# A recurrent GRU kernel: the input weights loaded in twelve 128-row chunks by GpSimd's queue, with the head of the program put in another order

## The chip, the cores and the metric

The kernel runs on one core of a Trainium2 chip. A core has five engines with instruction queues of their own: TensorE (PE in the profile; its weight loads are PEld), VectorE (DVE), ScalarE (ACT), GpSimd (POOL) and SyncE (SP). Each engine works through its queue in program order, and waits on semaphores where an operand comes from elsewhere. Transfers between the chip's memory (DRAM) and the on-chip memory (SBUF) are issued from the queues of SP, ACT or POOL and run on 16 DMA engines. Matmul results land in PSUM, which has eight banks.

The metric is the device time of one execution in microseconds. Less is better.

## The reference

A gated recurrent unit runs over 128 steps for a batch of 64, with 512 inputs and 512 hidden values, all in float32, and its outputs are added to x:

```
def step(h, inp):
    x_t, prop = inp
    comb = concatenate([x_t, h], -1)
    z = sigmoid(comb @ Wz + bz)
    r = sigmoid(comb @ Wr + br)
    comb2 = concatenate([x_t, r * h], -1)
    h_cand = tanh(comb2 @ Wh + bh)
    h_new = (1 - z) * h + z * h_cand
    h_next = where(prop, tanh(h_new @ Wp + bp), h_new)   # prop: every 4th step but the last
    return h_next, h_new
out = x + transpose(scan(step, h0, transpose(x)))
```

Each of Wz, Wr, Wh is 1024 x 512: the upper 512 rows multiply x and the lower 512 rows multiply h (or r * h). The state h0 is the input cond_1024.

## The kernel before

**Gates and halves.** The three gates are R, Z and H. `wx` holds the upper (x) halves of the three weight matrices as [128 partitions, 4 chunks k, 3 gates, 512], and `wh[R]`, `wh[Z]`, `wh[H_]` hold the lower (h) halves, one tile for each gate. Partition p = 32 q + e of chunk k holds row 128 q + 32 k + e of the matrix, for four quarters q. The batch is cut into two halves of 32. A gate's product for one half is four `products` (one for each chunk k), each of them two matmul calls, which the profile shows as four float32 matmuls 128x256. In this text a *unit* is one such `products` call: one chunk, one gate, one half, four matmuls. A recurrent gate (`gate`, L218) is four units for each half.

**Recurrent work.** `half(h)` (L782) is a generator that emits one half's steps: gate R, then rh = r * h_old and its transpose, gate Z, some fill, gate H, the new state and its transpose, some fill; and behind every fourth step a product with Wp. The loop at the end of the function runs the two generators against each other, the second one `LAG` = 700 columns behind, so that one half's products cover the other half's elementwise chain. The order that comes out is the order of every engine's queue; no scheduler changes it (`manual_schedule`).

**Fill work.** The products with x do not depend on the state. They stand in a list `queue`, `put` appends to it, and `fill(n, h)` takes the next n units for half h. `HEAD`, `PLACES` and `TAIL` hold how many units each step takes at its three places. For the first four steps these are plain products (`plain`, L434: three gates x four chunks for each half of the batch and step, in the PSUM tiles scratch_q and scratch_r for even steps, scratch_a and scratch_x for odd ones); `add_bias` (DVE, L417) then adds the bias into `cp`, and `seed` (ACT, L379) copies `cp` into the PSUM tile in which the recurrent gate accumulates. From step 4 on, groups of x products are done with fewer multiplications, by matmuls of 192 columns (`batch`): seven products stand for eight, on sums of blocks of x and of blocks of the weights.

**The sums that this needs.** Sums of x blocks: `sum_raw12(1)` makes the tile s12r, `sum_raw34(1)` the tile s34r, four POOL operations 128x128 each. Sums of weight blocks: `sum_inner(i, eng)` and `sum_inner_1(i, eng)` make, for factor i, four operands from four operations 128x384 (L297 to L302), and `sum_outer` (L288 to L290, six operations 128x768 into `tw`) and `sum_outer_1` (L294, two into `d5`) make the factors 4 to 7 out of `wx`. Step 1's fill is `batch((1, 0), ...)` on factors 1 and 2 with s12r; step 2's is `batch((1, 1), ...)` on factors 1, 5, 2 and 3 with s12r and s34r, then `batch((1, 2), ...)`; from step 3 on come the factors 6, 7 and 4.

**The head.** Ahead of step 0 the program is straight code. Transfers: x of steps 0 and 1 and all of `wx` on SP and ACT (`load_x`, L94; `load_w`, L100, one transfer for each quarter of 32 partitions); the biases, then h0, on POOL, which is held by a copy that waits for `wx`; x of steps 2 and 3 on SP; then `wh` on SP and ACT, and x of later steps and Wp on SP (`later_loads`). Compute: PE runs 40 fill matmuls on zeros (`idle`), spreads the biases over the partitions (`spread`, L181, with copies on ACT, L189), then 8 and 8 more fill matmuls around the transposes of x (`join_x`, DVE, L251). DVE turns h0 and makes the sums of factors 1 and 2 while POOL makes `d5` and the sums of 3 and 5. PE runs the plain products of steps 0 and 1, R of both, then Z of both, then H of both. Then the six `add_bias` (emitted when H of step 0 and of step 1 ends), the seeds, and step 0. In step 0 DVE runs `sum_outer`, and POOL `sum_raw12(1)` and the sums of 6.

Lines that the text names: L123 and L128 are the POOL transfers of biases and h0, L126 the copy into `held`, L610 `bias_d`, L757 the add of h to x, L551 and L546 sums of results, L799 rh, L838 and L847 the new state, L238 the transposes of states.

## Time and profile before

| | |
|---|---|
| median of 3 runs | 1277.14 us (1275.61 to 1277.23) |
| profiled execution | 1276.41 us, of which the profile's span is 1274.6 us |
| PE, PEld busy | 1253.5 us (98%), 1164.3 us (91%) |
| DVE, ACT, POOL busy | 781.5, 835.6, 886.8 us |
| mean granted PE clock | 0.994 of full speed |
| DMA | 60.82 MB, mean 48 GB/s |

A time line row has the start in microseconds from the span's beginning, the time from its first to its last instruction, the engine, the line, the operation, the output and inputs by tile name, the shape and the count; square brackets hold the idle time ahead of it and what ended it. Matmuls are pipelined, so the spacing of their starts, not the time of one, is what one costs. A row of waits has the waiting engine and operation, what released it, the sum in us, the number of waits and the longest. A window row has its length and each engine's busy time in it, then the clock that PE was granted (1.00 is full), the share of the 16 DMA engines' time that was busy (transfers that overlap on one engine can bring it over 1) and GB/s. A wait for several semaphores is put down to the one that came last by the profile, and may belong to another.

### The profile page before, as it was taken

The numbers are of one execution on the slowest core, as the hardware profiler recorded it, in microseconds if no ns is written. First come the engines' busy times: TensorE is split into PE (matmuls) and PEld (weight loads), VectorE is DVE, ScalarE is ACT, GpSimd is POOL, SyncE is SP. The second block draws the span as 40 slices with busy tenths as digits, with TensorE's granted clock in tenths as the row PEclk, the third lists the DMA queues.
The fourth block names the chain that finished last, engine by engine and source line by source line (L and its number), as shares of the span: only waits on it lengthen the run. The fifth ranks groups of instructions, "written<-read, shape, count | busy, mean of one in ns | idle before, by whom it ended". The sixth has DMA issues, their size and how long they took to land.

```text
span 1274.6 us, 60714 instructions
## 1 busy us (share of the span) xinstructions
PE 1253.5 (98%) x25968; PEld 1164.3 (91%) x25968; DVE 781.5 (61%) x2161; ACT 835.6 (66%) x2685; POOL 886.8 (70%) x1027
## 2 busy tenths in 40 slices
PE   6999999999999999999999999999999999999997
PEld 3699999999999999999999999999999999999875
DVE  4656666666666666666666665666666666666544
ACT  1456667666667666666766666666666666667665
POOL 5469767787677786777687677776777777677530
PEclk8999999999999999999999999999999999999999
DMA  8302212102121111112111121111111111111010
GB/s 225 83 20 53 52 37 54 49 22 52 51 54 36 34 46 44 52 36 54 36 34 52 49 54 39 32 40 52 52 37 36 52 37 52 40 49 36 9 46 19
DMA packets 113365, 60.82 MB, mean 48 GB/s; under 512 B 12969, under 2 KB 109481, under 8 KB 113097
## 3 DMA queue, kind: packets, MB, share of 16 engines
q1 hardware_dynamic: 110628, 53.46, 16.1%
q8 instruction: 205, 3.36, 1.2%
q10 hardware_dynamic: 2212, 3.34, 0.9%
q14 instruction: 64, 0.52, 0.1%
q0 software_dynamic: 256, 0.14, 0.1%
HBM read 40.11 MB, written 16.78 MB: 45 GB/s over the span
## 4 chain that ended last, share of the span: by engine, by line
PE 95%; DMA 2%; ACT 1%; issue 1%; DVE 1%; SPq 0%; ACTq 0%; POOLq 0%; POOL 0%; DVEq 0%
PE rec L209 44%; PE rec_z L209 16%; PE scratch_r L209 13%; PE scratch_q L209 10%; PE scratch_a L209 5%; PE scratch_y L209 4%; PE scratch_x L209 4%; DMA wx<-in_L_cond_Wh_dram 1%; DMA wh<-in_L_cond_Wh_dram 1%; SPq L94 0%; DMA wx<-in_L_cond_Wr_dram 0%; DMA wh<-in_L_cond_Wr_dram 0%; ACT rec_z L235 0%; ACT c L235 0%; DMA xr<-in_x_dram 0%
## 5 line engine op out<-in xcount | busy, mean ns | idle before, releaser
L209 PE MATMUL rec<-wh,rhT 128*32 128x256 f32 x4096 | 375.3, 379 | 0.1
L209 PE MATMUL rec<-wh,hT 128*32 128x256 f32 x3072 | 281.5, 379 | 1.3 <-DVE hT L238 1.3
L209 PE MATMUL rec_z<-wh,hT 128*32 128x256 f32 x3072 | 281.5, 379 | 0.1
L209 PEld LDWEIGHTS rec<-wh,rhT 128*32 128x32 f32 x4096 | 250.4, 110 | 20.0 <-ACT scratch_r L235 0.7
L235 ACT ACTIVATE scratch_r<-rec 64x128 f32<-64x128 f32 x512 | 128.0, 250 | 131.9 <-PE rec L209 67.9
L379 ACT COPY rec<-cp 64x256 f32<-64x256 f32 x512 | 189.9, 371 | 37.2 <-DVE cp L417 17.8
L209 PEld LDWEIGHTS rec<-wh,hT 128*32 128x32 f32 x3072 | 187.0, 110 | 15.2 <-ACT c L235 3.2
L209 PEld LDWEIGHTS rec_z<-wh,hT 128*32 128x32 f32 x3072 | 193.4, 110 | 7.3 <-ACT rec_z L379 0.6
L235 ACT ACTIVATE rec_z<-rec_z 64x128 f32<-64x128 f32 x512 | 128.0, 250 | 95.9 <-PE rec_z L209 83.8
L235 ACT ACTIVATE c<-rec 64x128 f32<-64x128 f32 x512 | 139.3, 272 | 62.2 <-PE rec L209 50.8
L757 POOL TENSOR_TENSOR xr<-xr,h 128x256 f32<-128x256 f32 x127 | 93.1, 734 | 93.1 <-DVE h L847 90.3
L546 POOL TENSOR_TENSOR mb<-mb,mb 128x768 f32<-128x768 f32 x58 | 106.2, 1831 | 66.9 <-DVE mb L512 66.9
L546 POOL TENSOR_TENSOR cp<-mb,mb 128x768 f32<-128x768 f32 x76 | 139.0, 1828 | 8.1 <-DVE mb L512 4.4
L546 POOL TENSOR_TENSOR cp<-mb 128x768 f32<-128x768 f32 x46 | 84.3, 1832 | 56.9 <-ACT rec_z L379 55.5
L813 DVE SCALAR_TENSOR_TENSOR keep<-rec_z,h 128x256 f32<-128x256 f32 x96 | 40.8, 425 | 133.6 <-ACT rec_z L235 130.5
L209 PE MATMUL scratch_r<-tw,s 128*32 128x192 f32 x928 | 120.9, 326 | 0.0
L485 ACT COPY cq<-scratch_q 128x384 f32<-128x384 f32 x212 | 102.1, 482 | 19.8 <-PE scratch_q L209 18.3
L502 DVE TENSOR_TENSOR cx<-scratch_r,cx 128x384 f32<-128x384 f32 x106 | 59.1, 558 | 80.6 <-PE scratch_r L209 69.3
L209 PE MATMUL scratch_q<-tt,s 128*32 128x192 f32 x928 | 103.7, 326 | 0.0
L508 DVE TENSOR_TENSOR mb<-scratch_q,cx 128x384 f32<-128x384 f32 x106 | 59.1, 557 | 57.9 <-ACT cq L485 57.7
L799 DVE TENSOR_TENSOR rh<-scratch_r,h 128x128 f32<-128x128 f32 x192 | 56.1, 292 | 60.0 <-ACT scratch_r L235 60.0
L209 PE MATMUL rec<-wh,hpT 128*32 128x256 f32 x992 | 91.4, 379 | 0.1
(182 smaller groups left out, 3823.9 us busy)
## 6 DMA issues: line engine op xcount, KB each, us to landing
out_dram<-xr SPq DMA_DIRECT2D x249, 64.0 KB, 1.8
xr<-in_x_dram SPq DMA_DIRECT2D x248, 64.0 KB, 2.1
xs<-in_x_dram SPq DMA_DIRECT2D x240, 64.0 KB, 2.2
wp<-in_L_cond_Wp_dram SPq DMA_DIRECT2D x4, 256.0 KB, 6.2
wx<-in_L_cond_Wr_dram SPq DMA_DIRECT2D x4, 128.0 KB, 3.1
wx<-in_L_cond_Wr_dram ACTq DMA_DIRECT2D x4, 128.0 KB, 3.6
wx<-in_L_cond_Wz_dram SPq DMA_DIRECT2D x2, 256.0 KB, 7.8
wx<-in_L_cond_Wz_dram ACTq DMA_DIRECT2D x2, 256.0 KB, 8.5
```

The lines of the kernel that those rows point to most:

```text
L209: nc.tensor.matmul(ps[part(2 * h + c)], lhsT=left, rhs=rhs(c), start=start, stop=True, skip_group_check=True,)
L235: nc.scalar.activation(dst[ts(d, 2 * V)], gate_ps(i, h)[ts(h, 2 * V), d, :], func)
L379: nc.scalar.copy(gate_ps(i, h)[rows].rearrange("p d (c n) -> p d c n", c=C), G[t][rows, :, :, i, :].rearrange("p c d n -> p d c n"),)
L485: nc.scalar.copy(c[:, :nm], ps[:, :nm])
L502: nc.vector.tensor_add(T2[what][:, :nm], r_ps[:, :nm], T2[what][:, :nm])
L508: nc.vector.tensor_add(blocks(1, 1), runs(q_ps[:, :nm]), runs(T2[what][:, :nm]))
L546: nc.gpsimd.tensor_add(dst, a, b)
L757: nc.gpsimd.tensor_add(xr[g][:, j], xr[g][:, j], h_new)
L799: nc.vector.tensor_mul(rh[:, h, :], r_, h_old[:, h, :])
L813: nc.vector.scalar_tensor_tensor(out=keep, in0=z, scalar=1.0, in1=h_old, op0=ALU.subtract, op1=ALU.mult)
```

## The change

**Loads.** The x half of each weight matrix comes in four transfers, one for each chunk k, each over all 128 partitions (256 KB), issued on POOL's queue: twelve in all, in the order R, Z, H. The biases move from POOL's queue to ACT's, h0 from POOL's to SP's ahead of x of steps 2 and 3. A memset on POOL writes one column of `wh[R]` behind the twelve issues; the transfers into `wh[R]` on SP and ACT have to wait for it. `wh[Z]` is issued behind the seeds of R, `wh[H_]` behind those of H.

**Order of the head.** The 16 fill matmuls and their places go. PE runs R of steps 0 and 1 first, then the spread of the biases, Z of both, H of both, and R of step 2. `add_bias` and the seeds of a gate follow that gate's products. Of the weight sums only those of factor 1 stay ahead of step 0 (on DVE).

**Weight sums.** In step 0, behind gate R, DVE makes those of 2; POOL, held by a copy that waits for them, makes those of 3 and `d5`, then behind gate Z s12r and the sums of 5; at the end of the step POOL makes `sum_outer`, which DVE did before. The sums of 6 move from step 0 to step 1, behind s34r, those of 7 from step 1 to step 3. Step 0 takes eight fill units for each half ahead of gate Z, and (4, 8, 0) instead of (12, 12, 0) at its places; x products of steps 2 and 3 are as many as before.

```
--- before.py
+++ after.py
@@ -114,25 +114,32 @@
     bias_p = const.tile([P, S, J], F32, name="bias_p")
     new_xr(0)
     load_x(xr[0], 0, 2, engs=both_queues)
-    for k in range(0, K, 2):
-        load_w(wx[:, :, R, :], gates_in[R][:D], k, k + 2, both_queues)
-    for i in (Z, H_):
-        load_w(wx[:, :, i, :], gates_in[i][:D], engs=both_queues)
-
+    for i in (R, Z, H_):
+        for k in range(K):
+            nc.gpsimd.dma_start(
+                out=wx[:, k, i, :],
+                in_=gates_in[i][:D].rearrange("(q k e) n -> k q e n", q=NQ, k=K)[k],
+            )
     for i, b in enumerate((br, bh, bz)):
-        nc.gpsimd.dma_start(out=bias_row[:, i, :], in_=b.rearrange("(o n) -> o n", o=1))
-
-    held = const.tile([1, 1], F32, name="held")
-    nc.gpsimd.tensor_copy(held, wx[0:1, 1, R, 0:1])
+        nc.scalar.dma_start(out=bias_row[:, i, :], in_=b.rearrange("(o n) -> o n", o=1))
+    nc.gpsimd.memset(wh[R][:, 0, 0:1], 0.0)
+
     for h in range(S):
-        nc.gpsimd.dma_start(
+        nc.sync.dma_start(
             out=h_init[:, h, :],
             in_=h0[ts(h, V), :].rearrange("b (q j) -> q b j", q=NQ),
         )
-    load_x(xr[0], 2, 2, 2)
 
     dummy = const.tile([1, 1], F32, name="dummy")
     nc.scalar.activation(dummy, ones[:, 0:1], AF.Sigmoid)
+
+    def load_wh(i):
+        load_w(wh[i], gates_in[i][D:], engs=both_queues)
+
+    load_x(xr[0], 2, 2, 2)
+    load_wh(R)
+
+    held = const.tile([1, 1], F32, name="held")
 
     xs = {}
 
@@ -142,8 +149,6 @@
             load_x(xs[g], g * Q4, Q4)
 
     def later_loads():
-        for i in range(3):
-            load_w(wh[i], gates_in[i][D:], engs=both_queues)
         new_xr(1)
         load_x(xr[1], Q4, Q4)
         load_xs(2)
@@ -285,9 +290,9 @@
 
     def sum_outer():
         for ka in range(S):
-            nc.vector.tensor_sub(tw[3][:, ka], outer(1, 1, ka), outer(0, 1, ka))
-            nc.vector.tensor_add(tw[2][:, ka], tw[3][:, ka], outer(0, 0, ka))
-            nc.vector.tensor_sub(tw[4][:, ka], outer(1, 0, ka), tw[2][:, ka])
+            nc.gpsimd.tensor_sub(tw[3][:, ka], outer(1, 1, ka), outer(0, 1, ka))
+            nc.gpsimd.tensor_add(tw[2][:, ka], tw[3][:, ka], outer(0, 0, ka))
+            nc.gpsimd.tensor_sub(tw[4][:, ka], outer(1, 0, ka), tw[2][:, ka])
 
     def sum_outer_1(eng):
         for ka in range(S):
@@ -437,7 +442,11 @@
             order = [(e, k) for k in range(K) for e in gates]
         return [
             plain_unit(
-                t, e, k, k == 0, *((lambda: add_bias(t, gates), gates) if (e, k) == order[-1] else ())
+                t,
+                e,
+                k,
+                k == 0,
+                *((lambda: add_bias(t, gates), gates) if t > 1 and (e, k) == order[-1] else ()),
             )
             for e, k in order
         ]
@@ -594,33 +603,11 @@
     PLACES = (
         (1, 7, 6), (1, 7, 0), (6, 8, 0), (6, 8, 0), (1, 8, 5), (1, 7, 0), (6, 8, 0), (6, 6, 0),
     )
-    HEAD = {0: (12, 12, 0), 1: (8, 6, 0), 2: (16, 12, 0), 3: (8, 6, 8), 4: (6, 8, 0)}
+    HEAD = {0: (4, 8, 0), 1: (8, 6, 0), 2: (16, 12, 0), 3: (8, 6, 8), 4: (6, 8, 0)}
     TAIL = {
         T - 10: (5, 9, 0), T - 9: (1, 7, 5), T - 8: (1, 7, 0), T - 7: (1, 5, 0), T - 6: (0, 5, 0),
         T - 5: (0, 4, 3), T - 4: (0, 5, 0), T - 3: (0, 4, 0), T - 2: (0, 4, 0), T - 1: (0, 0, 0),
     }
-
-    idle(40)
-    spread(scratch[3], slice(0, 2), (R, H_))
-    spread(scratch[1], slice(2, 3), (Z,))
-    join_x(0, 0)
-    idle(8)
-    join_x(0, 1)
-    idle(8)
-    nc.gpsimd.tensor_sub(bias_d, bias_x[:, 1], bias0)
-    later_loads()
-    hT = new_T("hT", "hT_init")
-    for h in range(S):
-        turn(hT[:, h, :], h_init[:, h, :])
-    for i in (1, 2):
-        sum_inner(i, nc.vector)
-        sum_inner_1(i, nc.vector)
-    sum_outer_1(nc.gpsimd)
-    for i in (3, 5):
-        sum_inner(i, nc.gpsimd)
-        sum_inner_1(i, nc.gpsimd)
-    put(sum(map(list, zip(*(plain(t)[:4] for t in range(2)))), []))
-    put(sum((plain(t)[n : n + 4] for n in (4, 8) for t in range(2)), []))
 
     def both(n):
         for _ in range(n):
@@ -628,11 +615,42 @@
                 for _ in fill(1, h):
                     pass
 
-    both(20)
-    for i in range(3):
-        for h in range(1 if i == Z else S):
-            seed(i, 0, h)
-    both(4)
+    def plain_two(i):
+        put(sum(map(list, zip(*(plain(t, (i,)) for t in range(2)))), []))
+        both(2 * K)
+
+    idle(40)
+    join_x(0, 0)
+    join_x(0, 1)
+    plain_two(R)
+    spread(scratch[3], slice(0, 2), (R, H_))
+    spread(scratch[1], slice(2, 3), (Z,))
+    for t in range(2):
+        add_bias(t, (R,))
+    for h in range(S):
+        seed(R, 0, h)
+    load_wh(Z)
+    nc.gpsimd.tensor_sub(bias_d, bias_x[:, 1], bias0)
+    hT = new_T("hT", "hT_init")
+    for h in range(S):
+        turn(hT[:, h, :], h_init[:, h, :])
+    plain_two(Z)
+    for t in range(2):
+        add_bias(t, (Z,))
+    seed(Z, 0, 0)
+    join_x(0, 2)
+    sum_inner(1, nc.vector)
+    sum_inner_1(1, nc.vector)
+    plain_two(H_)
+    for t in range(2):
+        add_bias(t, (H_,))
+    for h in range(S):
+        seed(H_, 0, h)
+    join_x(0, 3)
+    load_wh(H_)
+    later_loads()
+    put(plain(2) + plain(3))
+    both(K)
 
     state = {0: (h_init, hT)}
     made = {}
@@ -651,9 +669,7 @@
     def begin(t):
         u = (t - 3) % 8
         even = FIRST + 2 * ((t - 3) // 8)
-        if t == 0:
-            put(plain(2) + plain(3))
-        elif t == 1:
+        if t == 1:
             put(batch((1, 0), [(1, 1), (1, 2)]))
         elif t == 2:
             put(batch((1, 1), [(1, 10), (1, 11)]) + batch((1, 2), [(1, 8), (1, 9)]))
@@ -674,13 +690,12 @@
 
     def behind_r(t, duo, u):
         odd = FIRST + 2 * duo + 1
-        if t == 1:
-            sum_inner(7, nc.gpsimd)
-            sum_inner_1(7, nc.gpsimd)
         if t == 2:
             pair_left(0, 1, 2)
         elif t == 3:
             pair_right(0, 1, 10)
+            sum_inner(7, nc.gpsimd)
+            sum_inner_1(7, nc.gpsimd)
         if t == 4:
             sum_inner(4, nc.gpsimd)
             sum_inner_1(4, nc.gpsimd)
@@ -689,8 +704,13 @@
 
     def join(t, duo, u, n):
         even, odd = FIRST + 2 * duo, FIRST + 2 * duo + 1
-        if t == 0:
-            join_x(0, 2 + n)
+        if t == 0 and n == 0:
+            sum_inner(2, nc.vector)
+            sum_inner_1(2, nc.vector)
+            nc.gpsimd.tensor_copy(held, leftover(2)[0:1, 0, 0, 0:1])
+            sum_inner(3, nc.gpsimd)
+            sum_inner_1(3, nc.gpsimd)
+            sum_outer_1(nc.gpsimd)
         elif t == 1:
             join_x(1, 2 + n)
         elif t == 2:
@@ -709,6 +729,8 @@
         if t == T - 7:
             pair_left(0, 1, 2, LAST)
             pair_right(0, 1, 10, LAST)
+        if t == 0:
+            sum_outer()
         if t == 3:
             pair_left(1, 8, 9)
             pair_right(1, 8, 11)
@@ -805,6 +827,8 @@
             if h == 1:
                 join(t, duo, u, 0)
 
+            if t == 0:
+                yield from fill(2 * K, h)
             yield from gate(Z, h, hT, wh[Z])
             keep = new_two("keep", t)
             if h == 1:
@@ -816,15 +840,16 @@
                 join(t, duo, u, 1)
                 if t == 1:
                     sum_raw34(1)
+                    sum_inner(6, nc.gpsimd)
+                    sum_inner_1(6, nc.gpsimd)
                 if last:
                     nc.gpsimd.tensor_sub(xr[g][:, j], xr[g][:, j], keep)
                 if t == 0:
-                    sum_outer()
                     join_x(1, 0)
                     join_x(1, 1)
                     sum_raw12(1)
-                    sum_inner(6, nc.gpsimd)
-                    sum_inner_1(6, nc.gpsimd)
+                    sum_inner(5, nc.gpsimd)
+                    sum_inner_1(5, nc.gpsimd)
                 if t == 2:
                     for n in range(2, 4):
                         join_x(2, n)
```

## The prediction

> **What bounds the kernel now.** I read the page first, then the waits of TensorE (PE), then PE's time line and the windows over the first 100 us.
>
> ```profile
> span 1274.6 us, 60714 instructions
> PE 1253.5 (98%) x25968; PEld 1164.3 (91%) x25968; DVE 781.5 (61%) x2161; ACT 835.6 (66%) x2685; POOL 886.8 (70%) x1027
> ```
>
> PE is busy for 98% of the span, so time can only be won where PE stands still or runs slowly. The table of PE's waits over the whole span names two long ones.
>
> ```profile
> PE scratch_q L209 <- DMA xr<-in_x_dram: 5.3, 1, 5.3
> PE rec L209 <- ACT rec L379: 5.3, 1, 5.3
> ```
>
> Both lie in the head, which is the only part that the change touches. The windows (columns: window, length, busy time of PE, PEld, DVE, ACT, POOL, then the granted clock, DMA share and GB/s) show what each costs beside the wait: after it the clock is at one half.
>
> ```profile
> 10.00:15.00 5.00, 1.29 (x24) 0.63 (x16) 0.40 (x2) 1.97 (x5) 0.99 (x1) 0.95 1.05 259
> 15.00:20.00 5.00, 3.41 (x33) 1.87 (x37) 1.90 (x3) 0.00 (x0) 1.68 (x1) 0.50 0.62 187
> 20.00:25.00 5.00, 5.00 (x88) 3.04 (x84) 4.91 (x4) 0.00 (x0) 4.92 (x4) 0.87 0.94 270
> 30.00:35.00 5.00, 3.72 (x32) 1.72 (x36) 1.38 (x5) 1.55 (x5) 2.20 (x3) 0.50 0.75 154
> 35.00:40.00 5.00, 4.06 (x72) 2.22 (x68) 1.71 (x6) 2.74 (x10) 0.00 (x0) 1.00 0.69 162
> ```
>
> PE's time line gives the landmarks: R of steps 0 and 1 begins at 7.58, Z at 16.59, H (scratch_r, scratch_x) ends near 26, the first recurrent product runs at 31.28, step 1 begins at 49.78, step 2 at 59.51, and the first product that reads the sums s34r comes at 64.91.
>
> ```profile
> 4.96 1.06 PE L181 MATMUL scratch_x<-tt,ones 1*32 1x512 f32 x8
> 7.58 0.64 PE L209 MATMUL scratch_q<-wx,xT 128*32 128x256 f32 x8
> 16.59 3.64 PE L209 MATMUL scratch_q<-wx,xT 128*32 128x256 f32 x32 [5.30 <-DMA xr<-in_x_dram]
> 24.09 1.92 PE L209 MATMUL scratch_x<-wx,xT 128*32 128x256 f32 x32
> 31.28 3.64 PE L209 MATMUL rec<-wh,hT_init 128*32 128x256 f32 x28 [5.27 <-ACT rec L379]
> 49.78 0.39 PE L209 MATMUL rec<-wh,hT 128*32 128x256 f32 x2
> 59.51 0.39 PE L209 MATMUL rec<-wh,hT 128*32 128x256 f32 x2
> 64.91 0.33 PE L209 MATMUL scratch_y<-tt,s34r 128*32 128x192 f32 x1
> ```
>
> The wait at 16.59 is put down to x, but the product reads wx of gate Z, which landed then. The wait at 31.28 is VectorE's (DVE's) order: its bias adds (L417) stand behind eight sums over the weights.
>
> ```profile
> 18.29 0.56 DVE L297 TENSOR_TENSOR tt<-wx 128x384 f32<-128x384 f32 x1 [3.07 <-DMA xr<-in_x_dram]
> 28.05 1.34 DVE L302 TENSOR_TENSOR din<-wx 128x384 f32<-128x384 f32 x1
> 29.32 0.74 DVE L417 TENSOR_TENSOR cp<-scratch_q,bias_x 128x256 f32<-128x256 f32 x2
> ```
>
> **The change part by part.** I follow one clock, microseconds from the span's start, up to the landmark at 64.91; behind it both programs give PE the same work.
>
> *Loads of wx.* Sixteen transfers on two hardware queues become twelve of 0.262 MB on GpSimd's (POOL's). No row shows such a transfer. Issue: a POOL row of 128 short rows costs 0.70 us (h_init, two in 1.40), one row 0.48; the far end is 1.38, two ACT issues in 2.76 on a full queue. I take 0.70, the same number of rows: 1.3 + 12 x 0.70, POOL is free at 9.7. Transfer: between the rows at 241 and 398 GB/s.
>
> ```profile
> 5.88 1.40 POOL L128 DMA_DIRECT2D h_init<-in_cond_dram  x2
> 2.46 0.48 POOL L123 DMA_DIRECT2D tt<-in_L_cond_bz_dram  x1
> 16.45 2.76 ACTq L100 DMA_DIRECT2D wh<-in_L_cond_Wr_dram  x2
> 24.00:26.00 2.00, 2.00 (x40) 0.96 (x31) 1.90 (x3) 0.00 (x0) 1.92 (x2) 1.00 1.08 398
> 26.00:28.00 2.00, 0.01 (x3) 0.00 (x0) 1.97 (x2) 0.00 (x0) 2.00 (x3) 1.00 1.06 241
> ```
>
> Ahead of the last chunk go 3.15 MB of wx and 0.65 MB of x and h_init, from about 2.5. At 398 that ends at 12.0, at 241 at 18.3; with 1.05 MB of wh's R sharing the engines, 14.7 and 22.6. The fast row is one in which both halves of the partitions are written at once, as a chunk does, so I take the fast half of this: R by 8, Z by 11, H by 16.
>
> *Memset and wh.* The memset on wh[R] stands behind the twelve issues, so wh[R] is issued from 9.8 on SP and ACT, and behind it on ACT wait the bias copies and the seeds of R. ACT's wh loads of before landed 3.6 (R) to 8.0 us (H) after issue.
>
> ```profile
> wh<-in_L_cond_Wr_dram ACTq DMA_DIRECT2D x2, 256.0 KB, 3.6
> wh<-in_L_cond_Wh_dram ACTq DMA_DIRECT2D x2, 256.0 KB, 8.0
> 13.88 5.67 SPq L94 DMA_DIRECT2D xr<-in_x_dram  x8
> ```
>
> 9.8 + 0.8 + 8.0 = 18.6 is still ahead of the first reader at 20.5 below. Covered; with POOL issues of 1.38 the memset comes at 17.9, and the reader waits about 3 us. SP has ten issues ahead of wh[R] (h_init 2, x 8): at 5.67 / 8 = 0.71 each from 2.6 it is through at 9.7, no later than the memset. ACT's three bias issues land long before the spread at 10. ACT's half of wh[H] goes out last, behind the seeds of H at about 20.4, and lands between 24.9 and 29.3; its reader is 37 units into step 0, at 28.5 below. I count nothing, with 0.8 as the dear end.
>
> *The head on PE.* The price of a unit (one chunk of one gate for half the batch, four matmuls) is 0.215 us, from 16 matmuls in 0.86 in the chain of waits.
>
> ```profile
> 43.92 0.86 PE rec L209 x16
> 5.13 0.77 DVE L251 STREAM_TRANSPOSE xT<-xr 128x256 f32<-128x256 f32 x2 [3.98 <-DMA wx<-in_L_cond_Wr_dram]
> ```
>
> xT stood at 5.9 before; x now shares the engines with chunks, so R begins between 5.9 and the old 7.58; I take 6.7. Then 16 units of R (3.45), the bias spread (4.96 to 6.38 before, 1.4), 16 of Z, 16 of H, 8 of step 2's R (1.72): 6.7 + 3.45 + 1.4 + 3.45 + 3.45 + 1.72 + 0.3 for four starts = 20.5. Call this S0, the start of step 0; it was 31.28. The sixteen fill matmuls that go (two idle(8)) ran in 1.05 us inside a wait and are worth nothing. The eight DVE sums are no longer ahead of the adds (four are, 2.4 us, under PE's H).
>
> *Step 0 and 1.* Step 0 is 24 recurrent units and 40 fill units: 64 x 0.215 = 13.8. Step 1 is unchanged, 59.51 - 49.78 = 9.73. Step 2 begins at S0 + 23.5 and reaches s34r 5.4 later: PE is there at S0 + 28.9.
>
> *POOL's new queue.* This is what comes late next. In step 0 POOL is held (the copy to `held`) until DVE has made the sums of 2, which stand behind the second half's turned rh: 53.57 + 0.31 was 4.1 behind step 1's start, plus four sums of 0.6 gives S0 + 6.5. Then, by start-to-start times of these rows:
>
> ```profile
> 53.57 0.31 DVE L238 STREAM_TRANSPOSE rhT<-rh 128x128 f32<-128x128 f32 x1
> 47.15 0.46 POOL L310 TENSOR_TENSOR s12r<-xT 128x128 f32<-128x128 f32 x1 [14.88 <-DVE xT L251]
> 48.95 1.01 POOL L297 TENSOR_TENSOR tt<-tw 128x384 f32<-128x384 f32 x1
> 53.06 0.73 POOL L757 TENSOR_TENSOR xr<-xr,h 128x256 f32<-128x256 f32 x1
> 62.51 1.83 POOL L551 TENSOR_TENSOR mb<-mb,bias_x 128x768 f32<-128x768 f32 x1 [1.70 <-DVE mb L512]
> 64.42 1.83 POOL L546 TENSOR_TENSOR cp<-mb 128x768 f32<-128x768 f32 x1
> 18.32 4.31 POOL L294 TENSOR_TENSOR d<-wx 128x768 f32<-128x768 f32 x2 [5.24 <-DMA xr<-in_x_dram]
> ```
>
> a group of four sums 4.11 (48.95 to 53.06), a 128x768 operation 1.91, the s12r group 1.80, the add to xr 0.73. In program order: sums of 3, 4.11; sum_outer_1, 2 x 1.91; s12r, 1.80; sums of 5, 4.11; sum_outer, moved here from DVE, 6 x 1.91 = 11.46; xr, 0.73; three of s34r's four, 1.35. Together 27.4: s34r is ready at S0 + 33.9, and PE waits 33.9 - 28.9 = 5.0 us. The nearest dearer row is 2.15 for 128x768 beside DVE, which adds up to 2 us; nothing shows it cheaper. s12r itself is ready at S0 + 15.8, ahead of step 1's first fill, which stands behind 16 recurrent units, S0 + 13.8 + 3.4 = S0 + 17.2. What POOL still owes then (sums of 6 and 7) is read only from step 4 on and fits its idle time.
>
> *The clock.* A 5 us wait is as long as the two of before. These ran on at half clock to 21.3 and 35.0 (from the windows' clock shares), 4.7 and 3.7 us from their resumption; half of the mean 4.2 is lost, 2.1. The Trainium skill, "TensorE: Matmul & The Clock Gate", Part 1, has the full clock back after one busy window of about 3.4 us: that would make the loss 1.7 and my time 0.4 lower. Both rows here are longer, so the trace speaks for the larger one.
>
> *Sum.* S0 + 33.9 = 54.4 at s34r against 64.91: 10.5 won, 2.1 given to the clock, 8.4 net. The profiled execution took 1276.41, which is 0.73 under the median of 1277.14; 1276.4 - 8.4 = 1268.0.
>
> **Rivals.**
>
> *No wait on POOL* (0.12). If s34r is in time, PE's whole lead stays: step 2 at 44.0 against 59.51, 15.5 won, 1260.9. Against it: the eleven and a half us of sum_outer stand ahead of s34r in POOL's strict order, and only 5.0 of it would have to vanish. For it: nothing in the rows.
>
> *The loads come no faster* (0.15). The engines were already full (DMA share 1.05 at 10 to 15), and a third queue adds none. The last chunk at 22.6, then one chunk of units and the 2.0 behind it: S0 = 25.5, 5 later than mine, 1273.0. The Trainium skill, "DMA: Bandwidth & Descriptors", Issuing engines are not separate DMA queues, says just this: all queues interleave on the same sixteen engines. The trace agrees in part: the window 10 to 15 has 259 GB/s with three queues loaded, little over the 241, while 398 shows that the old rate was not the ceiling.
>
> *Slower: the chunks run on few engines* (0.14). The change breaks even where S0 is 28.9, that is, the last chunk at 26.0, or 134 GB/s. The ACT queue took 23.5% of 16 engines over 50 us for 3.28 MB, 57 engine-us per MB; 3.15 MB is 180. On sixteen engines that is 11 us, on the same four 45: S0 = 50.4, and the time 1298. Against it, the queue that POOL fills was on 31.6% of 16 = 5.1 engines in the window 10 to 11 us, with h_init's two transfers alone on it; for it, these took 8.0 us to land.
>
> ```profile
> q10 hardware_dynamic: 2080, 3.28, 23.5%
> q0 software_dynamic: 69, 0.07, 31.6%
> h_init<-in_cond_dram POOLq DMA_DIRECT2D x2, 64.0 KB, 8.0
> ```
>
> The same page, Why a DMA increments its semaphore by 16 and not by 1, has a transfer use as many engines as divide the slowest size of both sides: here four, the source's quarters, moving round from transfer to transfer. That would delay the first chunk and not the sum; more than four busy engines agrees with the moving.
>
> **How the numbers follow.** My forecast (1265 to 1270.5) has 0.53, no wait 0.12, loads no faster 0.15, slow chunks 0.14, and 0.06 is left for a mixture that lands within 0.2% (2.55 us, about what a measurement here can tell from no change). Faster: 0.53 + 0.12 + 0.15 = 0.80. The range runs from just under the no-wait time, 1260.5, up to 1277, where the slow chunks begin.
>
> **What would show it.** Right: the first recurrent product near 20.5; no wait of PE over 2 us ahead of it; POOL without a gap from about 27 to 56; one wait of about 5 us for s34r on POOL near 49; clock 0.5 behind it; step 3 some 8 us earlier. Wrong: PE waits between chunks ahead of 20 (loads), seeds of R behind the memset (POOL's issues), or no wait in step 2.

## The result, and the profile after

The changed kernel takes 1282.99 us (median; 1281.6 to 1284.06) against 1276.79 us for the kernel before on the same chip: a ratio of 1.0047, 95% interval 1.0035 to 1.006. It is slower, where 1268.0 was forecast. The execution that the profile shows took 1281.6 us.

```profile
span 1279.7 us, 60680 instructions
PE 1254.8 (98%) x25952; PEld 1161.4 (91%) x25952; DVE 769.1 (60%) x2155; ACT 835.1 (65%) x2685; POOL 899.7 (70%) x1041
```

PE's waits over the whole span (sum, number, longest) no longer hold the two long ones of before. Four that are new:

```profile
PE scratch_q L214 <- DVE cp L422: 4.5, 1, 4.5
PE scratch_y L214 <- POOL s34r L317: 3.8, 1, 3.8
PE scratch_q L214 <- DVE xT L256: 3.5, 1, 3.5
PE scratch_x L214 <- POOL s4r L317: 1.1, 1, 1.1
```

PE's time line gives the landmarks (products are on L214 now): R begins at 8.91, Z at 22.19, step 0 at 32.46, s34r is read at 67.03, step 3 begins at 77.31, s4r is read at 119.87.

```profile
8.91 1.08 PE L214 MATMUL scratch_q<-wx,xT 128*32 128x256 f32 x8 [3.52 <-DVE xT L256]
22.19 1.08 PE L214 MATMUL scratch_q<-wx,xT 128*32 128x256 f32 x8 [4.49 <-DVE cp L422]
32.46 1.93 PE L214 MATMUL rec<-wh,hT_init 128*32 128x256 f32 x28
67.03 0.54 PE L214 MATMUL scratch_y<-tt,s34r 128*32 128x192 f32 x2 [3.81 <-POOL s34r L317]
77.31 0.38 PE L214 MATMUL rec<-wh,hT 128*32 128x256 f32 x2
119.87 0.36 PE L214 MATMUL scratch_x<-tt,s4r 128*32 128x192 f32 x2 [1.08 <-POOL s4r L317]
```

Against before, the program is 1.2 us late at step 0 (31.28), 2.1 late at s34r (64.91), 3.5 late at step 3 (73.79) and 5.1 late at the end. It was ahead in between: step 1 begins at 47.90 (49.78 before). Step 0 is 3.1 us shorter: R of step 2, eight units or 1.7 us, is done ahead of it, and the kernel before ran the first 3.7 us of its step 0 at half clock, which cost 1.8; PE's waits inside the step are 1.4 against 0.9. In the kernel before PE has no wait for VectorE's sum_outer there.

The windows (PE, PEld, DVE, ACT and POOL busy, then granted clock, DMA share, GB/s) show low clock in four stretches. In the first three the DMA engines are full and move little; the fourth lies behind s34r:

```profile
10.00:15.00 5.00, 4.16 (x40) 1.53 (x36) 0.00 (x0) 0.00 (x0) 2.10 (x4) 0.50 1.07 148
15.00:20.00 5.00, 2.70 (x36) 0.74 (x28) 0.00 (x0) 0.00 (x0) 0.04 (x1) 0.84 1.17 172
20.00:25.00 5.00, 2.81 (x28) 1.38 (x32) 1.17 (x4) 1.67 (x5) 0.99 (x1) 0.50 1.01 178
65.00:70.00 5.00, 2.97 (x40) 1.88 (x44) 0.00 (x0) 0.00 (x0) 4.76 (x8) 0.66 0.34 94
```

The DMA queues over the first 50 us (packets, MB, share of 16 engines) and the issues of wx (KB each, median us to landing):

```profile
q0 software_dynamic: 3264, 3.16, 38.4%
wx<-in_L_cond_Wr_dram POOLq DMA_DIRECT2D x4, 256.0 KB, 9.9
wx<-in_L_cond_Wz_dram POOLq DMA_DIRECT2D x4, 256.0 KB, 15.5
wx<-in_L_cond_Wh_dram POOLq DMA_DIRECT2D x4, 256.0 KB, 14.4
```

By the trace's landings the four chunks of R are in by 14.0, those of Z by 21.5, those of H by 28.8. POOL's queue cost 38.4% of 16 engines over 50 us, 307 engine-us for 3.16 MB, or 97 per MB; the ACT queue of before cost 57. What stood behind the loads, on SP and ACT, and SP's longest wait:

```profile
5.68 13.63 SPq L94 DMA_DIRECT2D xr<-in_x_dram  x8
19.28 1.98 ACTq L100 DMA_DIRECT2D wh<-in_L_cond_Wr_dram  x2
21.30 0.65 ACT L194 COPY bias_x<-scratch_x 128x256 f32<-128x256 f32 x2 [11.33 <-issue]
SPq L94 <- DMA h_init<-in_cond_dram: 7.9, 2, 6.7
```

SP needs from 5.68 to 19.3 for eight issues of x; for 7.9 us of that it waits for h0 to land. wh's R is issued from 19.28 on. ACT's issue of it uses the completion semaphore of an x transfer that SP had issued at 6.05 and that landed at 19.2, so it waited for that landing. Only behind it does ACT copy the spread biases, at 21.30. POOL's queue:

```profile
39.96 0.17 POOL L710 COPY held<-din 1x1 f32<-1x1 f32 x1 [16.66 <-DVE din L307]
53.70 1.84 POOL L293 TENSOR_TENSOR tw<-wx 128x768 f32<-128x768 f32 x1
63.14 1.81 POOL L295 TENSOR_TENSOR tw<-wx,tw 128x768 f32<-128x768 f32 x1
65.58 0.45 POOL L315 TENSOR_TENSOR s34r<-xT 128x128 f32<-128x128 f32 x1
```

POOL stands idle for 16.66 us ahead of `held`, then has no gap up to s34r, and sum_outer (the first and the last of its six operations are shown) ends at 64.95, right ahead of s34r.

### The profile page after: what moved, and what is told of

Its sections match the earlier page's. It is cut to its first block, busy times and chain, and to the rows that moved or that the text cites. A ratio compares the mean times of both kernels' runs of the same rounds, so it can differ in the third digit from the quotient of the medians.

```text
span 1279.7 us, 60680 instructions
## 1 busy us (share of the span) xinstructions
PE 1254.8 (98%) x25952; PEld 1161.4 (91%) x25952; DVE 769.1 (60%) x2155; ACT 835.1 (65%) x2685; POOL 899.7 (70%) x1041
## 3 DMA queue, kind: packets, MB, share of 16 engines
q1 hardware_dynamic: 109996, 52.02, 15.5%
q0 software_dynamic: 3264, 3.16, 1.5%
## 4 chain that ended last, share of the span: by engine, by line
PE 91%; DMA 3%; POOL 3%; ACT 1%; SPq 1%; DVE 1%; issue 0%; ACTq 0%; POOLq 0%; DVEq 0%
PE rec L214 42%; PE rec_z L214 15%; PE scratch_r L214 13%; PE scratch_q L214 10%; PE scratch_a L214 5%; PE scratch_y L214 4%; PE scratch_x L214 4%; DMA h_init<-in_cond_dram 1%; DMA xr<-in_x_dram 1%; DMA wh<-in_L_cond_Wz_dram 1%; POOL cp L555 1%; POOL mb L560 1%; SPq L789 0%; DMA out_dram<-xr 0%; ACT rec_z L240 0%
## 5 line engine op out<-in xcount | busy, mean ns | idle before, releaser
L214 PE MATMUL rec<-wh,rhT 128*32 128x256 f32 x4096 | 375.5, 379 | 0.1
L214 PE MATMUL rec<-wh,hT 128*32 128x256 f32 x3072 | 281.6, 379 | 1.3 <-DVE hT L243 1.3
L214 PE MATMUL rec_z<-wh,hT 128*32 128x256 f32 x3072 | 281.6, 379 | 0.1
L214 PEld LDWEIGHTS rec<-wh,rhT 128*32 128x32 f32 x4096 | 249.5, 110 | 19.2 <-ACT scratch_r L240 0.5
L214 PEld LDWEIGHTS rec_z<-wh,hT 128*32 128x32 f32 x3072 | 192.4, 110 | 9.0 <-ACT rec_z L384 0.6
L214 PEld LDWEIGHTS rec<-wh,hT 128*32 128x32 f32 x3072 | 186.4, 110 | 14.2 <-ACT c L240 3.2
L214 PE MATMUL scratch_r<-tw,s 128*32 128x192 f32 x928 | 120.9, 326 | 0.0
L494 ACT COPY cq<-scratch_q 128x384 f32<-128x384 f32 x212 | 102.0, 481 | 19.8 <-PE scratch_q L214 18.4
L214 PE MATMUL scratch_q<-tt,s 128*32 128x192 f32 x928 | 103.6, 326 | 0.0
L214 PE MATMUL rec<-wh,hpT 128*32 128x256 f32 x992 | 91.4, 379 | 0.1
## 6 DMA issues: line engine op xcount, KB each, us to landing
wx<-in_L_cond_Wz_dram POOLq DMA_DIRECT2D x4, 256.0 KB, 15.5
wx<-in_L_cond_Wh_dram POOLq DMA_DIRECT2D x4, 256.0 KB, 14.4
```

The costliest lines, as they stand in the source:

```text
L214: nc.tensor.matmul(ps[part(2 * h + c)], lhsT=left, rhs=rhs(c), start=start, stop=True, skip_group_check=True,)
L494: nc.scalar.copy(c[:, :nm], ps[:, :nm])
```

## The experiments

All times are medians; ratios are against the kernel before on the same chip, whose median lay between 1276.49 and 1277.07. The landmarks come from one profiled execution each, and its time can differ from the median by up to 2.6 us (e2), so they are compared inside an execution.

| | step 0 | step 3 | span | time | ratio (95%) |
|---|---|---|---|---|---|
| before | 31.28 | 73.79 | 1274.6 | 1276.8 | |
| changed | 32.46 | 77.31 | 1279.7 | 1283.0 | 1.0047 (1.0035 to 1.006) |
| e1 chunks on SP and ACT | 50.73 | 94.74 | 1297.1 | 1299.5 | 1.018 (1.016 to 1.02) |
| e2 128 rows in one run | 28.83 | 73.68 | 1276.3 | 1275.5 | 0.9993 (0.9983 to 1.0002) |
| e3 loads of before | 30.06 | 74.20 | 1276.7 | 1279.6 | 1.002 (1.0011 to 1.003) |
| e4 s34r first | 34.23 | 73.47 | 1279.4 | 1281.3 | 1.0034 (1.0022 to 1.0046) |
| e5 sum_outer on DVE | 34.08 | 81.18 | 1284.0 | 1285.4 | 1.0066 (1.0049 to 1.0083) |
| e6 quarters on POOL | 31.11 | 75.28 | 1277.8 | 1281.1 | 1.0034 (1.0023 to 1.0046) |
| e7 and wh's R on SP | 30.53 | 77.01 | 1280.4 | 1280.6 | 1.003 (1.0017 to 1.0044) |
| e8 e7 and sum_outer on DVE | 30.54 | 79.99 | 1283.3 | 1284.9 | 1.0059 (1.0044 to 1.0074) |
| e9 quarters, POOL let go | 35.28 | 73.56 | 1274.7 | 1276.9 | 1.0001 (0.9991 to 1.001) |
| e10 e7 and h0 on POOL | 28.30 | 72.37 | 1275.7 | 1277.7 | 1.0008 (0.9999 to 1.0018) |
| e11 e10 and POOL let go | 27.64 | 65.92 | 1268.0 | 1270.0 | 0.9946 (0.9931 to 0.9961) |
| e12 e11 with the chunks | 40.63 | 78.90 | 1280.9 | 1284.4 | 1.006 (1.0044 to 1.0077) |

**e1: the chunks on the hardware queues.** Is it the form of a chunk, led by its four quarters, that makes it slow?

```
-            nc.gpsimd.dma_start(out=wx[:, k, i, :], ...)
+            both_queues[k % 2].dma_start(out=wx[:, k, i, :], ...)
```

> The twelve chunk transfers of the changed kernel as they are, but issued alternately on SP and ACT instead of POOL. Theory A (the form: a chunk's source leads with four quarters, so each transfer runs on four engines only): the hardware queues put them no faster, and if they always take the same four engines 3.15 MB at 57 engine-us per MB need 45 us, step 0 starts near 50 and the time is 1295 to 1300. Theory B (POOL's queue: its packets are dearer whatever the form): the chunks land by about 18 as the loads of before did, step 0 starts near 23, 1270 to 1273. Theory C (the order of the head loses by itself): no change, 1280 to 1284.

1299.5 us. A window of this run (DMA share and GB/s at its end):

```profile
20.00:30.00 10.00, 0.00 (x0) 0.00 (x0) 0.00 (x0) 0.00 (x0) 0.00 (x0) 0.50 0.26 102
```

and PE's longest wait in it:

```profile
PE scratch_x L186 <- DMA tt<-in_L_cond_bh_dram: 18.4, 1, 18.4
```

Twelve chunks on SP and ACT keep 0.26 of the sixteen engines busy, about four, at 102 GB/s, and the other twelve do nothing. With eight transfers in flight more would be busy if each took other engines, so they were the same four. PE waits 18.4 us for a bias of 2 KB that stands behind them. The form does confine a transfer. That step 0 begins near 50, as theory A had it, is in part luck: by the trace's landings the last chunk was in at 37.3, where the theory's 45 us from the first issue would end near 48; the rest is the spread, Z and H, which stood behind the bias. The Trainium skill, "DMA: Bandwidth & Descriptors", Why a DMA increments its semaphore by 16 and not by 1, has a hardware queue use the lowest-numbered engines, as many as divide the slowest size of both sides, and GpSimd's queue as many from a place that moves on. Both runs agree: 0.26 here, 1.07 to 1.17 in the changed kernel.

**e2: chunks of 128 rows in one run**, still on POOL's queue.

```
-                in_=gates_in[i][:D].rearrange("(q k e) n -> k q e n", q=NQ, k=K)[k],
+                in_=gates_in[i][k * P : (k + 1) * P],
```

> Chunk k takes 128 rows in a row of the matrix instead of four groups of 32, all else as in the changed kernel, POOL's queue too. The product then pairs rows of x and of the weights wrongly; the work and the bytes are the same. Theory A (form): 16 engines share each transfer, the last chunk lands by 16 to 18 instead of 28.8, step 0 starts at 21 to 24 instead of 32.5, 1270 to 1273 with the wait for s34r left. Theory B (queue): the chunks land as late as now, 1281 to 1284. Theory C: the loads get faster and the time stays at 1280 or more.

1275.5 us, between theory A and theory C. The same queue and bytes over the same 50 us:

```profile
q0 software_dynamic: 960, 3.15, 18.7%
```

and PE's longest wait:

```profile
PE scratch_q L211 <- DVE cp L419: 5.0, 1, 5.0
```

The queue's cost is half: 18.7% of 800 is 150 engine-us, 47 per MB, with 960 packets in place of 3264. The 2304 that are gone are packets of 8 bytes, 192 to a chunk; the 4096-byte packets that carry the data took 160 ns in the median, against 292 ns in the changed kernel. H is in by 15.4 instead of 28.8, very near the 16 that the prediction had. Yet step 0 begins at 28.83, not 20.5: PE waits 5.0 us ahead of Z for `add_bias` of R. Fast loads alone are not enough.

**e3: the loads of before** (sixteen quarter transfers on SP and ACT), all else changed.

```
-        for k in range(K):
-            nc.gpsimd.dma_start(out=wx[:, k, i, :], ...)
+    for k in range(0, K, 2):
+        load_w(wx[:, :, R, :], gates_in[R][:D], k, k + 2, both_queues)
+    for i in (Z, H_):
+        load_w(wx[:, :, i, :], gates_in[i][:D], engs=both_queues)
```

> The changed kernel with the input weights loaded as before (sixteen quarter transfers on SP and ACT), so the new order alone. Theories A and B: the weights land near 18 as before, step 0 starts at 22 to 25, PE then waits 4 to 5 us for s34r, 1270 to 1274. Theory C: the bias copies, held on ACT behind wh[R], keep Z of steps 0 and 1 from running, step 0 starts at 30 or later, 1280 or more.

1279.6 us, 5.6 over the first theory's range and just short of the rival's. Step 0 begins at 30.06, as the rival had it, but PE's longest wait is another:

```profile
PE scratch_x L184 <- DMA tt<-in_L_cond_bh_dram: 4.4, 1, 4.4
```

Now the biases, which stand behind the weights on ACT's queue, hold PE for 4.4 us. The new order of the issues costs time whichever way the weights come.

**e4: s34r ahead of sum_outer.**

```
         if t == 0:
-            sum_outer()
...
                 if t == 1:
                     sum_raw34(1)
+                    sum_outer()
```

> The changed kernel with sum_outer on POOL moved from the end of step 0 to step 1, behind s34r. All theories of the loads: step 0 starts as late as now (32.5). If the 3.8 us of PE's wait for s34r and the half clock behind it are lost time, both go: 1281.6 - 3.8 - 1.7 = 1276. Rival: POOL's next debts (the sums of results that step 4's seeds read) are due as late, and the wait moves there: 1280 to 1282.

1281.3 us: the rival. The wait at s34r is gone, and step 3 comes 39.2 us behind step 0 (44.9 in the changed kernel). But step 4 then comes 16.7 behind step 3 (14.1), and step 5 11.4 behind step 4 (9.7). The chain, from PE back to ACT:

```profile
88.82 0.36 PE L214 MATMUL scratch_q<-wx,xT 128*32 128x192 f32 x2 [2.40 <-DVE mb L517]
87.30 0.38 ACT L384 COPY rec_z<-cp 128x256 f32<-128x256 f32 x1 [3.86 <-POOL cp L555]
```

ACT's seed waits 3.86 us for a result that POOL makes late, DVE waits behind ACT, PE behind DVE, and the clock halves again. POOL's debt was moved, not paid; step 0 also began 1.8 later than in the changed kernel in this execution.

**e5: sum_outer back on VectorE** in step 0.

```
-            nc.gpsimd.tensor_sub(tw[3][:, ka], outer(1, 1, ka), outer(0, 1, ka))
...
+            nc.vector.tensor_sub(tw[3][:, ka], outer(1, 1, ka), outer(0, 1, ka))
...
```

> The changed kernel with sum_outer back on VectorE, at its place in step 0 of the kernel before; all else as changed. Theory C (the six 128x768 sums that GpSimd got stand ahead of s34r, 6 x 1.91 = 11.5 us, and make both the wait at s34r and the later one at s4r): the first recurrent product stays near 32.5, the wait for s34r (3.8) and the half clock behind it (1.7) go, and so does the 1.1 at s4r; 1283.0 - 6.6 = 1276.4, 1275 to 1278. Rival (the debt is only handed to VectorE, whose turned states then come late): the gain is under 2 us, 1281 to 1283, and a wait on VectorE of 3 us or more stands in steps 0 to 4.

1285.4 us, worse than the changed kernel: the theory fell, and the loss is more than its rival had. PE's waits:

```profile
PE rec L214 <- DVE hT L243: 8.2, 5, 6.6
PE scratch_x L214 <- POOL s4r L317: 1.1, 1, 1.1
```

and, from the time line, DVE's first and last operation of sum_outer:

```profile
44.46 1.54 DVE L293 TENSOR_TENSOR tw<-wx 128x768 f32<-128x768 f32 x1
52.89 0.96 DVE L295 TENSOR_TENSOR tw<-wx,tw 128x768 f32<-128x768 f32 x1
```

s34r is in time, but DVE turns the new state only behind sum_outer's 9.4 us (5.8 in the kernel before), and PE waits 6.6 for it. So in the changed order, with the sums of 2 in step 0 too, VectorE has no room for sum_outer there. And the 1.1 us at s4r stays although POOL is rid of sum_outer. What is left to cause it are the sums of 7, which the change puts into step 3; e9 and e11, which put them back into step 1 among other things, have no wait at s4r.

**e6: quarters on POOL's queue.**

```
-        for k in range(K):
-            nc.gpsimd.dma_start(out=wx[:, k, i, :], ...)
+        load_w(wx[:, :, i, :], gates_in[i][:D], engs=(nc.gpsimd, nc.gpsimd))
```

> The changed kernel with the weights of x still on GpSimd's queue, in twelve transfers of the same bytes, but each of them one quarter of a gate's rows for 32 partitions (as the kernel before loads Z and H) and not one chunk over all 128. Theory A (the form of the chunk, led by its four quarters, holds a transfer on few engines): landings as with 128 rows in one run, R by 8.5, H by 15.5, and 1275 to 1277. Rival D (GpSimd's queue is slow for any transfer of rows that go to 32 partitions): H lands at 24 or later and the time is 1282 or more. Either way VectorE's bias adds, behind the biases' copies on ScalarE, hold the products of Z for 3 us or more, and s34r is waited for.

1281.1 us: neither range. The queue's cost is 24.8% of 800, 63 engine-us per MB:

```profile
q0 software_dynamic: 960, 3.15, 24.8%
```

but PE's waits stay:

```profile
PE scratch_q L210 <- DVE cp L418: 4.1, 1, 4.1
PE scratch_y L210 <- POOL s34r L313: 4.0, 1, 4.0
```

Both were forecast for this run, and they are about as long as in the changed kernel; the quicker loads have nothing to show for it but 1.9 us. By the trace's landings R is in by 10.3 and H by 19.6 (8.5 and 15.5 expected, 14.0 and 28.8 in the changed kernel). But R begins at 10.40, 1.5 later than in the changed kernel, because its first product needs all four quarters, where one chunk was enough.

**e7: and wh's R on SyncE alone**, so that ACT's copies stand behind no transfer.

```
-    load_wh(R)
+    load_w(wh[R], gates_in[R][D:])
```

> As the kernel with quarters on GpSimd's queue, and all four transfers of wh's R issued by SyncE, none by ScalarE, so that ScalarE's copies of the biases stand behind no transfer that waits. Theory B (the products of Z wait for add_bias of R, which waits for those copies): PE's wait ahead of Z falls from 4 to 5 us to 1.5 or less, the first recurrent product comes 3 to 4 us earlier, near 25, and the time is 3 to 4 us less than with quarters alone, 1271 to 1273; the wait for s34r stays, as GpSimd's queue starts with step 0. Rival (the copies are late for another cause, the biases' own landing or the spread): the wait stays over 3 us and the time is that of the quarters alone.

1280.6 us, 7.6 over the range. The wait ahead of Z falls from 4.1 to 0.5, so its cause is shown; the time does not follow, as the next wait takes its place:

```profile
PE scratch_q L210 <- DVE cp L418: 0.5, 1, 0.5
PE rec L210 <- DMA wh<-in_L_cond_Wr_dram: 2.8, 1, 2.8
```

Its cause is in SP's time line and waits:

```profile
5.83 14.93 SPq L94 DMA_DIRECT2D xr<-in_x_dram  x8
SPq L94 <- DMA h_init<-in_cond_dram: 11.5, 2, 6.3
```

SP's eight issues of x take until 20.8, 11.5 us of that waiting for h0 to land, and wh's R goes out behind them.

**e8: e7, and sum_outer on VectorE** as in e5.

> As the kernel before this one, and sum_outer on VectorE in step 0. If the three causes are separate and add: the first recurrent product near 25, no wait of 2 us at s34r, 1265 to 1268, faster than both kernels. If VectorE becomes the bound instead: 1270 to 1273, with a wait on VectorE in steps 0 to 3.

1284.9 us: 17 over the first case and 12 over the second, whose wait on VectorE is there. What e5 showed holds here too:

```profile
PE rec L210 <- DVE hT L239: 8.4, 5, 6.7
```

Up to here no mend pays, neither alone nor with the others. What remained was POOL's idle time in the head, and the issues of SP.

**e9: POOL let go in the head** (on e6).

```
-            nc.gpsimd.tensor_copy(held, leftover(2)[0:1, 0, 0, 0:1])
...
+    # ahead of step 0, behind the seeds of H:
+    sum_inner(3, nc.gpsimd); sum_inner_1(3, nc.gpsimd)
+    sum_outer_1(nc.gpsimd)
+    sum_inner(5, nc.gpsimd); sum_inner_1(5, nc.gpsimd)
+    sum_outer((0,))                 # the other half stays behind step 0
...
+    # t == 1, behind the sums of 6: the sums of 7, out of step 3
```

> As the kernel with quarters on GpSimd's queue (1281.1), with GpSimd let go in the head: the copy to held is out, the sums of 3, sum_outer_1, the sums of 5 and the first half of sum_outer stand directly behind the seeds of H, ahead of step 0; the second half of sum_outer stays behind step 0, and the sums of 7 go back to step 1, behind those of 6. No sum is added or left out. Theory C' (GpSimd stood idle for some 16 us of the head, between bias_d and held, and that idle time is what it owes at s34r and s4r): no wait at s34r (4.0), none at s4r (1.1), full clock in step 2 (1.7): 1274 to 1276. Rival (GpSimd's sums beside VectorE's in the head slow the bias adds, or the wait comes up again at another reader): 1278 or more, with a wait of 2 us or more on VectorE or GpSimd.

1276.9 us, some 1 above the expectation. Step 3 comes 38.3 us behind step 0 (44.2 in e6), the waits at s34r and s4r are gone. The rest is in the head, which is 4.2 later in this execution: PE's wait ahead of Z has the clock at half behind it, and DVE's sums beside POOL's take longer than the 0.56 that the same line takes in the changed kernel:

```profile
29.77 2.07 DVE L297 TENSOR_TENSOR tt<-tt,wx 128x384 f32<-128x384 f32 x1
```

**e10: h0 on POOL's queue** (on e7), behind wx's R.

```
-        nc.sync.dma_start(out=h_init[:, h, :], ...)
...
+        if i == R:
+            for h in range(S):
+                nc.gpsimd.dma_start(out=h_init[:, h, :], ...)
```

> As the kernel with wh's R issued by SyncE alone (1280.6), and the first state's two transfers go to GpSimd's queue behind the four of wx's R, where SyncE issued them ahead of x of steps 2 and 3. Theory E (SyncE's issues of x, and behind them wh's R, stood from 5.8 to 20.8 because they waited for the first state's landing, which took some 14 us beside the weights): SyncE is through with x by 14 and wh's R lands by 22; the wait of 2.8 for wh goes, the first recurrent product comes at 25 to 28, and the time is 1276 to 1278. Rival (the engines are full and the order of the issues changes nothing): the first recurrent product stays at 30 or later, 1280 or more.

1277.7 us, as expected: 2.9 less than e7. SP's time line:

```profile
0.75 10.37 SPq L94 DMA_DIRECT2D xr<-in_x_dram  x12
```

and the wait that is left:

```profile
PE scratch_y L210 <- POOL s34r L313: 4.0, 1, 4.0
```

SP is through with x at 11.1 instead of 20.8, and wh no longer holds step 0, which begins at 28.30, just past the 25 to 28 that were expected.

**e11: e10 with POOL let go.**

> As the kernel before this one, with GpSimd let go in the head as well (no held, its sums of 3 and 5, sum_outer_1 and half of sum_outer ahead of step 0). If the causes are separate and add: first recurrent product at 25 to 28, no wait at s34r or s4r, 1269 to 1271, faster than both kernels. If not, 1274 or more, with the wait that took over on VectorE, on GpSimd or on wh's Z.

1270.0 us, as expected, and faster than both kernels: 0.9946 (0.9931 to 0.9961). The page's first line:

```profile
span 1268.0 us, 60680 instructions
```

PE's two longest waits:

```profile
PE scratch_q L208 <- DMA wx<-in_L_cond_Wr_dram: 5.1, 1, 5.1
PE rec L208 <- DVE hT L237: 1.7, 4, 0.8
```

POOL's first sum, which dates the last transfer of H:

```profile
21.46 1.01 POOL L296 TENSOR_TENSOR tt<-wx 128x384 f32<-128x384 f32 x1 [2.72 <-DMA wx<-in_L_cond_Wh_dram]
```

and POOL's queue over the first 50 us (h0's two transfers with it):

```profile
q0 software_dynamic: 1120, 3.28, 29.3%
```

Behind the first load no single wait of PE is over 1.0 us. R's first three groups still run at half speed (0.85 us apart, 0.43 later); from 13.4 on the clock stays full up to the last 2 us.

**e12: the chunks put back into e11.**

> As the mended kernel (1270.0), with the twelve transfers over all 128 rows of the changed kernel back in place of the quarters; nothing else. This gives the price of the chunk's form where the waits behind it are mended. If the last chunk of H lands near 27, as it did in the changed kernel (28.8, with the first state on SyncE's queue beside it), one chunk of units and 2.0 follow, so that the first recurrent product comes at 30 to 31 instead of 27.6: 1272.5 to 1274. If the form were the main loss of the changed kernel, 1277 or more; if the waits were all of it, under 1271.

1284.4 us: 14.4 more than e11, which is the case "main loss", and not the 2.5 to 4 that were expected. The same three views:

```profile
PE scratch_r L212 <- DMA wx<-in_L_cond_Wh_dram: 6.8, 3, 4.0
```

```profile
38.08 1.00 POOL L300 TENSOR_TENSOR tt<-wx 128x384 f32<-128x384 f32 x1 [15.34 <-DMA wx<-in_L_cond_Wh_dram]
```

```profile
q0 software_dynamic: 3424, 3.30, 42.4%
```

H is complete at 38.0 instead of 21.4. The expectation took the landing from the changed kernel; but there wh's R was issued from 19.3 on, and here from 16.5, while H's chunks were under way, and a chunk of H took 20.3 us in the median (14.4 there). That they lost the engines to wh is the likely reading, but not shown: h0's two transfers also stand ahead of Z's and H's chunks on POOL's queue here, and H's were issued at 13.6 to 15.7 (8.0 to 14.3 in the changed kernel). No run parts wh and h0 from the other traffic. The waits for H then halve the clock as well.

## Why the prediction was wrong, point by point

*What bounds the kernel*: right. All but 0.3 of the 5.1 us stands at step 7 (121.84 against 117.04), and behind it both programs run alike. But 1.3 of it come after the landmark at 64.91 and the half clock there, at s4r, where the prediction counted nothing.

*Loads of wx*: the step that failed first. "The fast row is one in which both halves of the partitions are written at once, as a chunk does, so I take the fast half" gave R by 8, Z by 11, H by 16; measured 14.0, 21.5 and 28.8. Even the slow bound, 241 GB/s, was too fast: the engines ran at 148 to 178 GB/s while full. The rival "chunks run on few engines" named the mechanism, four at a time, but set it aside because moving round "would delay the first chunk and not the sum". e1 shows the four, and e2 that the sum was doubled, 97 engine-us per MB against 47. Its break-even (last chunk at 26.0, S0 at 28.9) was missed by 2.8 and 3.6 us on the slow side; 1276.4 + 3.6 = 1280.0 would have been its time, against 1281.6 profiled. The 134 GB/s that it names for this break-even counts wx alone; with the 0.65 MB of x and h0 that its own sum has ahead of the last chunk it is 162, in the middle of the measured 148 to 178.

*POOL's issues*: 0.7 each as taken, but three of the last four waited 5.2 us in all for earlier chunks to land, and the memset came at 14.9, not 9.7.

*"Covered"* (memset and wh): wrong. SP was not through at 9.7 but at 19.3: the 0.71 for an issue had no wait in it, and its issues of x waited 7.9 for h0. ACT's half of wh's R waited as long, for the landing of one of these x transfers (in e2, e6 and e9 the table of waits names such a landing ahead of ACT's copies, with 8.2, 11.7 and 12.2 us). That put the biases' copies, behind it on ACT, at 21.3. The prediction saw the copies wait there and did not ask who waits for them: Z of steps 0 and 1 goes into the PSUM tiles that `add_bias` of R reads, so PE waited 4.5. e7 shows the cause.

*The head on PE*: 20.5 against 32.46, 12.0 late. R began 2.2 late (8.91 for 6.7). R of 16 units took 7.2 us, to the spread at 16.14, instead of 3.45: 0.8 of the 3.8 is a wait for R's second chunk, the rest half clock. From there to Z it took 6.0 in place of 1.4 for the spread and 0.3 for starts (4.4, the wait for `add_bias`), and half clock made Z 5.1 long (1.6). Together 12.0. H's chunks held nothing here: H's products ran at 27.28 to 30.73, just behind the landings. The faults hid behind each other. Quarters in place of chunks gave 1.9 us with the waits as they were (changed to e6) and 14.4 with the waits mended (e12 to e11); the mended waits gave nothing with chunks (1283.0 to 1284.4) and 11.1 with quarters (e6 to e11). e2 gave 7.5 with the waits as they were, as its chunks let R begin at 7.28.

*POOL's new queue*: right in place and size. s34r was ready at S0 + 34.5 (33.9 forecast); PE waited 3.8 (5.0), since it came later itself, step 2 at S0 + 25.2 (23.5); 1.4 of that is a wait for rh in step 0, which the sum of units leaves out.

*The clock*: 1.4 lost behind s34r (2.1 forecast). The clock record of the trace has half clock from 66.45 to 69.86, 3.4 us, of which PE ran 2.8; step 3 is 1.4 later against before than s34r is. The one busy window of about 3.4 us of the Trainium skill, "TensorE: Matmul & The Clock Gate", Part 1, comes near this, and near the 3.3 us of half clock behind the wait ahead of Z; it does not give the 6.3 us from the start of R, which have a wait of 0.8 in them. What was left out is that slower loads bring waits, and so half clock, ahead of step 0 as well.

*"What POOL still owes ... fits its idle time"*: wrong by 1.1 at s4r, in every run but e4 that kept the sums of 7 in step 3; e5 rules out sum_outer as its cause. The larger error of this part was to take the held POOL as given: its 16.66 us of idle time ahead of `held` were what it lacked later, and letting it go, with the sums of 7 back in step 1, gave 4.1 us (e6 to e9) and 7.7 (e10 to e11).

The sum: S0 came 12.0 later and s34r 12.6 later than forecast. Less the 0.7 that the clock did not take, and with 1.1 at s4r and some 0.6 in small differences, that turns 8.4 won into 5.2 lost on the profiled executions (1276.41, 1281.6).

The price of a chunk can be split by the packet records of the traces. The chunks cost 157 engine-us more than e2's rows: 128 of it are the 4096-byte packets, which took longer, and 28 the packets of 8 bytes. Four engines alone are not the reason. In e1 the chunks ran on four engines too, and their packets of 2048 bytes took 84 ns, 42 engine-us per MB, less than the 57 of the ACT queue before; and in e6 quarters without packets of 8 bytes took 258 ns for 4096 bytes. Why the 4096-byte packets of POOL's queue take so long stays open: other transfers ran beside them in each case, and no run had the chunks alone.

## What to carry to other kernels

Before a transfer is reshaped, look at the outermost size of both its sides: a chunk over all partitions that is led by four quarters used four engines at a time, and on POOL's queue cost twice the engine time of the same bytes as 128 rows in one run. When an issue moves to another queue, follow what its landing releases, the issues behind it and the engine's own work behind those, up to PE; here small transfers of h0 held x, x held wh, and wh held a bias copy. An engine that is held back while it has nothing to lose pays later: work that moves to it needs idle time that was found in the trace, at the place where it is done.

## What the runs showed of the hardware that was not expected

On SP's and ACT's queues all twelve chunks stayed on about four engines (0.26 of sixteen at 102 GB/s); on POOL's the same chunks kept all sixteen busy (1.07 to 1.17) but each brought 192 packets of 8 bytes.

An issue can stand for a long time for a transfer that is none of its operands: SP's eight issues of x took 13.63 us in the changed kernel and 14.93 in e7, 7.9 and 11.5 of it waiting for h0, and POOL's ninth chunk waited for its first. In the trace of the changed kernel the transfers of SP and ACT share eight completion semaphores, POOL's use eight others, and each issue waits for the landing of the transfer that had its semaphore before.

By the clock records a stretch at half clock, idle time included, lasted a multiple of 3.4 us: 3.4, 6.8, in e12 also 10.2, and 23.9 in e1, where PE stood for 18.4. Counted from where PE resumed behind a wait of 2.8 to 6.7 us, half clock lasted between 2.7 us (e4, e6) and 6.3 us (changed kernel). The length of the wait does not set it: behind a wait of 4.1 us it was 2.7 in e6, behind one of 4.0 it was 5.4 in e7.
